# Row scatters and residual traffic handed out over heads and chunks, each behind a one-element copy in GpSimd's queue

## The chip, the cores and the metric

The kernel runs on one core of one Trainium2 chip. The metric is the device time of one execution in microseconds, as the median of several runs. A core has five instruction queues: PE (TensorE, matrix products), DVE (VectorE), ACT (ScalarE), POOL (GpSimd) and SP (SyncE, which here only issues DMAs). POOL issues DMAs too, the indirect ones among them. All DMAs of a core are carried by its 16 DMA engines.

## The reference

The kernel computes one transformer block on 4 sequences of 512 tokens with 512 features (B, S, D). A cross attention comes first, then causal self-attention with 16 heads, then a mixture of 16 experts of which each token takes 6, beside a shared expert. Cut to what matters:

```python
x = x + x_attention(layernorm(x), ctx_1024)        # softmax(q k^T) from ctx alone
h = rmsnorm(layernorm(x), ln1_w)
q, k, v = h @ wq, h @ wk, h @ wv                   # 16 heads of 128
attn = softmax(where(causal, q k^T / sqrt(128), -1e9))
x2 = layernorm(x) + (attn v) @ wo
h2 = rmsnorm(x2, ln2_w)
topv, topi = top_k(softmax(h2 @ gate_w.T), 6)      # topv normalized to sum 1
routed = sum over the 6 experts e of topv_e * (silu(h2 @ eg_e.T) * (h2 @ eu_e.T)) @ ed_e.T
shared = (silu(h2 @ sg.T) * (h2 @ su.T)) @ sd.T
out = x + x2 + routed + shared
```

The residual that ends up in the output is thus the sum of two tensors: `x` after the cross attention (in the kernel `x1`) and `x2` after the self-attention. Its sum is what the change calls the rest.

## The kernel before

**Number format.** Each float32 operand is held as two float16 halves (hi and lo), and each product is three matmuls (`mm3`, lines 83, 86 and 87 of the kernel before).

**Stages.** Batches are called b = 0 to 3. `xattn(b)` is the cross attention, a generator whose pieces are run between other work. The main loop runs over n, one (batch, head) pair per turn, from a list `heads` of 64 pairs. In turn n the queries and keys of head n are made, its scores and softmax follow, and head n-1 is multiplied with its values by `attend`, which leaves `ao` (written by ACT, then by DVE). Two heads form a group; when both are attended, `project` adds their part of the output projection to `x2`. The list goes through batches 0 and 1 in turn, group by group, then through 2 and 3. Batch 0's last heads are 24 and 25, batch 1's 32 and 33, batch 2's 56 and 57, batch 3's 60 to 63.

**Routing.** When a batch's last group is projected, three steps follow. `route1(b)` (same turn) normalizes `x2` tile by tile, splits it into `h2p` (hi by ACT, lo by POOL for batches 0 to 2, line 78), turns it by a DMA transpose (`flip`, line 91, on SP's queue) into `h2T`, and for each of the four tiles does the residual work: load a tile of `x1` from DRAM into `x1t` (one buffer), add `x2`, store it to `r_d` (lines 489, 490, 491, all on POOL). `route2(b)` (two turns later) computes gates, and `route3(b)` (three turns later) the slot of each (token, expert) pair in DRAM, `slotu`, and lists 24 scatters per batch in `scat`: 4 tiles of 128 tokens by 6 experts.

**Scatters.** `scatter(n)` takes up to n entries from that list and issues for each one an indirect DMA from POOL, 128 rows of 2 KB from `h2p` into the expert-sorted array `xs_d` in DRAM (line 455). The main loop calls `scatter(8)` each turn; the last batch's are all issued at once after `route3(B - 1)`. They are declared to be without dependencies among each other, because their slots differ.

**After the loop.** `shared_down(0)`, then `shared(1)`, `shared(2)`: the shared expert in six chunks of up to 128 columns (`gate_up`, leaving `hs`) and a down projection over four tiles (`shared_down`, which adds to `acc`, loaded from `r_d`). `rows_in` then loads rows of `xs_d` by DMA transpose for the first expert, and the 16 experts follow. Results go to `y_d` and are gathered back by indirect DMAs on POOL (line 1105). Batch 3's shared expert stands at the end.

**Order.** A planner with a simulated timeline puts the instructions of each engine in order. `after(b, a)` asks it to keep b behind a on a queue, and `pin` to keep program order. [...] POOL's queue carries, besides the above, the loads of attention weights from their DRAM copies (`fetch`, line 413: `wqk`, `wv`, `wo`), of the shared expert's weights (line 449: `shst`), the stores and loads of `x1` and `hid` (lines 338, 355, 655), and parts of the normalization and routing.

The lines in question, as they stand before:

```python
        scatter(8)
        shared_weights()
...
            x1t = xp.tile([P, D], F32, tag="x1t", name="x1t", bufs=1)
            nc.gpsimd.dma_start(x1t, x1_d[b][:, t, :])
            nc.gpsimd.tensor_tensor(x1t, x1t, x2[:, t, :], ALU.add)
            nc.gpsimd.dma_start(r_d[b][:, t, :], x1t)
```

Of the kernel before, what the change touches and what calls it, by code (L numbers as in the profile page):

```python
# [9 lines left out]
F16 = mybir.dt.float16  # L10
F32 = mybir.dt.float32
# [6 lines left out]
P = 128  # L18
B, S, D = 4, 512, 512
# [36 lines left out]
def xattn_moe_block_kernel(ctx: ExitStack, tc: tile.TileContext, x, xT, ctxT, wqkx, bqk, ln1, ln2,  # L56
# [33 lines left out]
    def flip(o, i):  # L90
        return nc.sync.dma_start_transpose(out=o, in_=i)

    def after(ins, first):
        tc.add_manual_dep(ins.ins, first.ins.name,
                          mybir.DependencyInfo(mybir.DependencyClass.NoSync, mybir.DependencyReason.DATA),
                          reason="order on the queue")
# [341 lines left out]
    def shared_weights():  # L438
# [6 lines left out]
        if pieces:  # L445
# [3 lines left out]
            pin(nc.gpsimd.dma_start(st_, src))  # L449
            loaded.append((dst, st_))  # L450

    def scatter(n):
        while scat and n:
            tt, k = scat.pop(0)
            ins = nc.gpsimd.indirect_dma_start(  # L455
                out=xs_d, out_offset=bass.IndirectOffsetOnAxis(ap=slotu[:, tt, k:k + 1], axis=0),
                in_=h2ps[tt], in_offset=None)
            tc.declare_no_dep(ins.ins, group="scat", reason="the slots differ")
            tc.add_to_no_dep_group("scat", ins.ins)
            scats.append(ins)  # L460
            n -= 1

# [8 lines left out]
    def route1(b, x2):  # L471
        ms = bsm.tile([P, NT], F32, name="rms")
        for t in range(NT):
            sq = xp.tile([P, D], F16, tag="h2", name="rsq", bufs=1)
            nc.scalar.activation(sq, x2[:, t, :], AF.Square, scale=1.0 / math.sqrt(D),
                                 accum_out=ms[:, t:t + 1])
        rr = bsm.tile([P, NT], F32, name="rrs")
        rsqrt(rr, ms, 1e-6)
        h2T[b] = hpool.tile([P, 2 * C, S], F16, tag="hT", name=f"h2T{b}")
        for t in range(NT):  # L480
            tt = b * NT + t
            tl = slice(t * P, (t + 1) * P)
            h2 = xp.tile([P, D], F32, tag="h2", name="h2", bufs=1)
            nc.vector.scalar_tensor_tensor(h2, x2[:, t, :], rr[:, t:t + 1], ln2b, ALU.mult, ALU.mult)
            h2p = h2ps[tt] = rp.tile([P, 2 * D], F16, tag="h2p", name="h2p", bufs=4)
            split1(h2p[:, :D], h2p[:, D:], h2, nc.vector if b == B - 1 else nc.gpsimd)
            zz["flip"] = flip(h2T[b][:, :, tl], h2p)
            x1t = xp.tile([P, D], F32, tag="x1t", name="x1t", bufs=1)
            nc.gpsimd.dma_start(x1t, x1_d[b][:, t, :])
            nc.gpsimd.tensor_tensor(x1t, x1t, x2[:, t, :], ALU.add)  # L490
            nc.gpsimd.dma_start(r_d[b][:, t, :], x1t)

# [180 lines left out]
    def gate_up(b, hid, tmp):  # L673
        shw = shx["w"]
        hs = []
        for ic in range(6):
            R = P if ic < 5 else SR
            if ic % 3 == 0:
                hs.append(hid().rearrange("p (i a s) -> p i a s", i=3, a=2))
            h = hs[-1][:, ic % 3]  # L680

            def proj(ps, a):
                o0 = ic * 8 * P + a * C * P
                mm3(ps, [(shw[:, 0, o0 + c * P:o0 + (c + 1) * P], shw[:, 1, o0 + c * P:o0 + (c + 1) * P],
                          h2T[b][:, c], h2T[b][:, C + c]) for c in range(C)])

            t = tmp()
            pg = bank("a", f"sg{b}_{ic}")
            proj(pg, 0)
            if ic < 5:  # L690
                zz["silu", b, ic] = nc.scalar.activation(t, pg, AF.Silu, scale=PSC)
                pu = bank("w", f"su{b}_{ic}")
                proj(pu, 1)
                nc.vector.scalar_tensor_tensor(t, pu, GS * PSC, t, ALU.mult, ALU.mult)
            else:
                nc.scalar.activation(t[R:], pg[:R], AF.Silu, scale=PSC)
                nc.vector.scalar_tensor_tensor(t[:R], pg[R:], GS * PSC, t[R:], ALU.mult, ALU.mult)
            zz["hs", b] = split1(h[:R, 0], h[:R, 1], t[:R])
            if ic == 5:
                nc.scalar.activation(h[R:2 * R, 0], t[:R], AF.Copy)  # L700
            yield hs

    def store(tt, acc):
        nc.sync.dma_start(out[tt // NT, (tt % NT) * P:(tt % NT + 1) * P, :], acc)

    def shared_down(b, hs, last=False):
        sdw = shx["d"]
        acc = residual(b)
        for t in range(NT):
            tl = slice(t * P, (t + 1) * P)  # L710
            ps = bank("s", f"sy{b}_{t}")
            mm3(ps, [(hs[ic // 3][:, ic % 3, 0, tl], hs[ic // 3][:, ic % 3, 1, tl],
                      sdw[:, 0, ic * D:(ic + 1) * D], sdw[:, 1, ic * D:(ic + 1) * D]) for ic in range(5)], stop=False)
            nc.tensor.matmul(ps, hs[1][:, 2, 0, tl], sdw[:, 0, 5 * D:], start=False, stop=False)
            nc.tensor.matmul(ps, hs[1][:SR, 2, 1, tl], sdw[:SR, 0, 5 * D:], start=False, stop=True)
            nc.vector.scalar_tensor_tensor(acc[:, t], ps, 1.0 / (GS * WS), acc[:, t], ALU.mult, ALU.add)
            if last:
                store(b * NT + t, acc[:, t])

    early = gate_up(0, lambda: ht.tile([P, 2 * NT, S], F16, tag="pt", name="hs0").rearrange("p k s -> p (k s)")[:, :6 * S],  # L720
                    lambda: stg.tile([P, 1024], F32, tag="st", name="sg0")[:, :S])
# [5 lines left out]
        path += [(b + i, g) for g in range(2) for i in range(1, 3) if b + i < B]  # L727
    partner.update((p, q) for p, q in zip(path, path[1:]) if p[1] == q[1])
    heads = [(b, g * HG + j) for b, g in path for j in range(HG)]
    opened = set()  # L730
    left = {b: G for b in range(B)}
    agenda = {}
# [2 lines left out]
    for n in range(NH + LAG + 1):  # L735
        if n < NH:
            b, h = heads[n]
            if b not in opened:
                opened.add(b)
                step(b, 99)  # L740
                if b == B - 1:
                    shared_pool()
            parts = [queries(b, h)]
            if h % HG == 0:
                parts.append(values(b, h // HG))
            if n == 0:
                parts.reverse()
                for p in parts:
                    next(p)
            for p in parts:  # L750
                for _ in p:
                    pass
        m = n - LAG
        if n >= NH:
            for _ in range(3):
                hs0 = next(early)
        if ready:
            b, g = ready.pop()
            project(b, g)
            left[b] -= 1  # L760
            if not left[b]:
                route1(b, x2s[b])
                agenda[n + 2] = agenda[n + 3] = b
                if stop == "B":
                    nc.sync.dma_start(out[b].rearrange("(t p) d -> p t d", p=P), x2s[b])
        if n < NH:
            scores(*heads[n])
        if 0 <= m < NH:
            b, h = heads[m]
            attend(b, h)  # L770
            if h % HG == HG - 1:
                ready.append((b, h // HG))
        if n in agenda and n < NH:
            b = agenda[n]
            if n + 1 in agenda:
                route2(b)
            else:
                route3(b)
        scatter(8)
        shared_weights()  # L780
        if H // 2 <= n < H // 2 + E:
            pad_rows(n - H // 2)
        if n < 6:
            step(1, 2)
        else:
            for _, j in zip(range(2 - n % 2), bring):
                step(j)
    if stop == "B":
        return
    shared_down(0, hs0)  # L790
    bctx.close()
    st2 = ctx.enter_context(tc.tile_pool(name="st2", bufs=2, side="right", reuse_waits="tile"))

    def shared_up(b, tick=lambda: None):
        for hs in gate_up(b, lambda: st2.tile([P, 6 * S], F16, name="hs"), lambda: st2.tile([P, S], F32, name="sgt")):
            tick()
        return hs

    def shared(b):
        shared_down(b, shared_up(b))  # L800

    route2(B - 1)
    route3(B - 1)
    scatter(B * NT * K)

    cps = bank("s", "cnt")
    nc.tensor.matmul(cps[:, :E], onesm, macc, start=True, stop=True)
# [121 lines left out]
    def rows_in(e, h):  # L929
        lo, n = h * CUT, CAPS[e] - CUT if h else CUT  # L930
        t = xts[e, h] = xin.tile([P, 2 * C, n], F16, tag="xT", name="xT")
        flip(t, xs_d[bass.ds(here[e] * T + (1 + lo), n), :])

    seat(0)
    nxt = ranked_weights(0)
    rows_in(0, 0)
    rows_in(0, 1)
    shared(2)

    N = B * NT * K  # L940
    sf, tf = (v.rearrange("p t k -> p (t k)") for v in (slot, tid))
# [185 lines left out]
    def tick():  # L1127
        left = ring["steps"]
        ring["steps"] = max(left - 1, 1)
        for _ in range(-(-len(todo) // left)):  # L1130
            gather()
# [18 lines left out]
    flush()  # L1150
    want(K - 1, yrc, cws, y_d)
    ring["steps"] = 5
    hs = shared_up(B - 1, tick)
    add(0)
    shared_down(B - 1, hs, last=True)
    late.clear()
# [72 lines left out]
```

## Time and profile before

| what | value |
|---|---|
| median of 3 runs | 1832.03 us (1832.01 to 1837.33) |
| profiled execution: time / span | 1838.93 / 1837.2 us |
| PE busy / DVE / ACT / POOL | 1739.6 / 1113.9 / 829.5 / 444.8 us |
| mean granted TensorE clock | 0.974 of full speed |
| `xs_d` scatters (line 455) | 96, 95.3 us of POOL |
| `x1t` loads, adds, stores (lines 489 to 491) | 16 each |
| DMA traffic | 296.23 MB, 161 GB/s on average |

The page of a profile gives busy times of the engines, then the span in 40 equal slices (45.9 us each) with the busy share in tenths, then DMA queues, a chain of waits and groups of instructions. Answers about the trace add a timeline, tables of windows and a list of who waited for whom. In the timeline a line gives start, length, engine, line of the kernel, operation, output and inputs, shapes, a count, and in brackets the idle time before it with what ended it; "issue" there is idle time in which the engine waited for nothing that the profile shows. A busy PE is not a PE at its peak, since the ends of matmuls are modelled. All times of stages below are microseconds from the start of the span.

### The profile page before, as it was taken

How to read it: one execution, taken by the hardware profiler on the slowest of the kernel's cores; microseconds unless marked ns; L12 is line 12 of the kernel's file. 1: busy time of each engine (PE TensorE's matmuls, PEld its weight loads, DVE VectorE, ACT ScalarE, POOL GpSimd, SP SyncE). 2: the span in 40 equal slices, each digit the busy share in tenths (PEclk: the TensorE clock that was granted, in tenths of full speed). 3: DMA queues.
4: the chain of work that ended last, by engine and by line, in shares of the span. 5: the costliest groups of instructions: out<-in, count | busy, mean ns of one | idle time of the engine just before them, and what ended most of it. 6: DMA issues, size and time to landing. Idle time of an engine off the chain costs nothing. (4 is left out here: it accounts for less than half of the span.)

```text
span 1837.2 us, 27581 instructions
## 1 busy us (share of the span) xinstructions
PE 1739.6 (95%) x9919; PEld 937.2 (51%) x9919; DVE 1113.9 (61%) x2766; ACT 829.5 (45%) x1711; POOL 444.8 (24%) x522
## 2 busy tenths in 40 slices
PE   7899999999986998999999979899999999999998
PEld 3455555555543554645655534345555555555453
DVE  6887777777673774756667625554444434446755
ACT  4555645465432543535445423234444444544431
POOL 5423011130345235000003334400000000025564
PEclk9899999999997998999999989899999999999999
DMA  7977768674675677654437534566454655579766
GB/s 235 228 165 215 160 144 191 159 185 93 136 161 159 151 168 212 134 101 91 86 68 150 130 107 102 199 178 177 138 155 144 178 147 147 148 223 252 217 206 209
DMA packets 392723, 296.23 MB, mean 161 GB/s; under 512 B 334880, under 2 KB 335136, under 8 KB 391808
## 3 DMA queue, kind: packets, MB, share of 16 engines
q1 hardware_dynamic: 359456, 180.32, 42.0%
q0 software_dynamic: 33120, 114.06, 19.6%
q8 instruction: 80, 1.31, 0.3%
q14 instruction: 67, 0.55, 0.1%
HBM read 124.81 MB, written 88.94 MB: 116 GB/s over the span
## 5 line engine op out<-in xcount | busy, mean ns | idle before, releaser
L1105 POOL DMA_INDIRECT yg<-y_d,yrc x96 | 110.5, 1151 | 535.8 <-DVE hf L1008 455.6
L630 ACT ACTIVATE pe<-pe,bnm 128x128 f32<-128x128 f32 (+3 forms) x256 | 142.4, 557 | 161.1 <-DVE bnm L628 156.4
L83 PE MATMUL qk<-hT,wqk 128*128 128x512 f16 (+1 forms) x520 | 197.8, 380 | 5.0 <-DMA hT<-hh 3.8
L86 PE MATMUL qk<-hT,wqk 128*128 128x512 f16 (+1 forms) x520 | 197.9, 381 | 1.1 <-issue 1.1
L87 PE MATMUL qk<-hT,wqk 128*128 128x512 f16 (+1 forms) x520 | 197.8, 380 | 1.1 <-issue 1.1
L74 DVE SCALAR_TENSOR_TENSOR pn<-pe,brc,pn 128x128 f16<-128x128 f32 (+3 forms) x256 | 146.7, 582 | 21.9 <-ACT pn L73 18.6
L628 DVE CUSTOM_DVE_ANT_0 pe<-sc,causal 128x128 f32<-128x128 f32 (+3 forms) x256 | 117.4, 486 | 64.0 <-PE sc L625 57.2
L86 PE MATMUL v<-wv,hT 128*128 128x256 f16 x512 | 141.6, 276 | 6.5 <-issue 6.5
L83 PE MATMUL v<-wv,hT 128*128 128x256 f16 x512 | 141.5, 276 | 6.4 <-issue 5.5
L73 ACT ACTIVATE pn<-pe,brc 128x128 f16<-128x128 f32 (+3 forms) x256 | 133.5, 553 | 30.1 <-ACT pe L630 16.3
L87 PE MATMUL v<-wv,hT 128*128 128x256 f16 x512 | 141.5, 276 | 4.9 <-issue 4.7
L83 PE MATMUL g<-xT,wt 128*128 128x384 f16 (+2 forms) x384 | 127.3, 331 | 0.0
L86 PE MATMUL g<-xT,wt 128*128 128x384 f16 (+2 forms) x384 | 127.3, 331 | 0.0
L87 PE MATMUL g<-xT,wt 128*128 128x384 f16 (+2 forms) x384 | 127.2, 331 | 0.0
L994 ACT ACTIVATE hT_e<-hf 128x384 f16<-128x384 f32 (+3 forms) x96 | 51.1, 532 | 143.9 <-DVE hf L1008 136.2
L73 ACT ACTIVATE qkt<-qk 128x512 f16<-128x512 f32 x128 | 75.0, 588 | 90.5 <-PE qk L87 85.0
L83 PE MATMUL y<-dt,hT_e 128*128 128x512 f16 (+1 forms) x288 | 109.4, 380 | 0.0
L87 PE MATMUL y<-dt,hT_e 128*128 128x512 f16 (+1 forms) x288 | 108.9, 378 | 0.0
L86 PE MATMUL y<-dt,hT_e 128*128 128x512 f16 (+1 forms) x288 | 108.9, 378 | 0.0
L662 DVE SCALAR_TENSOR_TENSOR x<-wo,x 128x512 f32<-128x512 f32 x128 | 87.5, 687 | 32.5 <-PE wo L87 31.4
L74 DVE SCALAR_TENSOR_TENSOR qkt<-qk,qkt 128x512 f16<-128x512 f32 x128 | 87.7, 686 | 28.6 <-ACT qkt L73 24.0
L455 POOL DMA_INDIRECT xs_d<-h2p,slotu x96 | 95.3, 993 | 28.2 <-issue 28.2
(320 smaller groups left out, 4019.8 us busy)
## 6 DMA issues: line engine op xcount, KB each, us to landing
y_d<-yt SPq DMA_DIRECT2D x96, 256.0 KB
est<-in_ew_dram SPq DMA_DIRECT2D x32, 704.0 KB
est<-in_ed_dram SPq DMA_DIRECT2D x16, 768.0 KB
wqk<-wqk_d POOLq DMA_DIRECT2D x20, 512.0 KB
wqk_st<-in_wqk_dram SPq DMA_DIRECT2D x16, 512.0 KB
wqk_d<-wqk POOLq DMA_DIRECT2D x15, 512.0 KB
xs_d<-causal POOLq DMA_DIRECT2D x16, 384.0 KB
wv<-wv_d POOLq DMA_DIRECT2D x10, 512.0 KB
```

The source lines that it names most:

```text
L73: return (nc.scalar.activation(hi, src, AF.Copy, scale=scale), nc.vector.scalar_tensor_tensor(lo, src, scale, hi, ALU.mult, ALU.subtract))
L74: nc.vector.scalar_tensor_tensor(lo, src, scale, hi, ALU.mult, ALU.subtract))
L83: ins = nc.tensor.matmul(o, lh, rh, start=start and j == 0, stop=False)
L86: nc.tensor.matmul(o, lh, rl, start=False, stop=False)
L87: ins = nc.tensor.matmul(o, ll, rh, start=False, stop=stop and j == n - 1)
L455: ins = nc.gpsimd.indirect_dma_start(out=xs_d, out_offset=bass.IndirectOffsetOnAxis(ap=slotu[:, tt, k:k + 1], axis=0), in_=h2ps[tt], in_of ...
L628: nc.vector.tensor_tensor_reduce(pe, ps[:, :w], causal[:, S - w:], -1.0, 3e38, ALU.add, ALU.min, nm)
L630: nc.scalar.activation(pe, pe, AF.Exp, bias=nm, scale=-1.0, accum_out=sm)
L662: nc.vector.scalar_tensor_tensor(x2[:, t, :], ps, 1.0 / (VS * WS), x2[:, t, :], ALU.mult, ALU.add)
L994: nc.scalar.activation(hT[:R, ic, :w], hf, AF.Copy)
L1105: nc.gpsimd.indirect_dma_start(out=yg, out_offset=None, in_=src, in_offset=bass.IndirectOffsetOnAxis(ap=idx[:, tt, k:k + 1], axis=0))
```

## The change

Three things are done. First, `pace(src)` puts a copy of one element into POOL's queue, from a tile that another engine writes into a tile `mark`, and asks the planner to keep it behind the last scatter or mark; `scatter` and the `x1` load ask to be kept behind the last mark in turn. Second, the residual work leaves `route1`: each (batch, tile) is put on a list `rest`, and `rest_step` does one of them per turn of the main loop; what is left after the loop is done tile by tile in `shared_down(0)`. Third, the scatters of a turn are no longer 8 but the number left, divided by the turns until the next batch ends (`ends`); batch 3's are handed out two per chunk and per tile in `shared(1)` and `shared(2)` (`drip`), and the remaining ones, with the loads of the first expert's rows, are issued after the second chunk of `shared(2)`. The mark of turn n reads `ao` of head n-2.

```diff
@@ -449,6 +449,14 @@
             pin(nc.gpsimd.dma_start(st_, src))
             loaded.append((dst, st_))
 
+    mark = const.tile([1, 1], F16, name="mark")
+
+    def pace(src):
+        ins = nc.gpsimd.tensor_copy(mark, src)
+        if scats:
+            after(ins, scats[-1])
+        scats.append(ins)
+
     def scatter(n):
         while scat and n:
             tt, k = scat.pop(0)
@@ -457,6 +465,8 @@
                 in_=h2ps[tt], in_offset=None)
             tc.declare_no_dep(ins.ins, group="scat", reason="the slots differ")
             tc.add_to_no_dep_group("scat", ins.ins)
+            if scats:
+                after(ins, scats[-1])
             scats.append(ins)
             n -= 1
 
@@ -485,8 +495,17 @@
             h2p = h2ps[tt] = rp.tile([P, 2 * D], F16, tag="h2p", name="h2p", bufs=4)
             split1(h2p[:, :D], h2p[:, D:], h2, nc.vector if b == B - 1 else nc.gpsimd)
             zz["flip"] = flip(h2T[b][:, :, tl], h2p)
+            rest.append((b, t, x2))
+
+    rest = []
+
+    def rest_step():
+        if rest:
+            b, t, x2 = rest.pop(0)
             x1t = xp.tile([P, D], F32, tag="x1t", name="x1t", bufs=1)
-            nc.gpsimd.dma_start(x1t, x1_d[b][:, t, :])
+            ins = nc.gpsimd.dma_start(x1t, x1_d[b][:, t, :])
+            if scats:
+                after(ins, scats[-1])
             nc.gpsimd.tensor_tensor(x1t, x1t, x2[:, t, :], ALU.add)
             nc.gpsimd.dma_start(r_d[b][:, t, :], x1t)
 
@@ -703,7 +722,7 @@
     def store(tt, acc):
         nc.sync.dma_start(out[tt // NT, (tt % NT) * P:(tt % NT + 1) * P, :], acc)
 
-    def shared_down(b, hs, last=False):
+    def shared_down(b, hs, last=False, tick=lambda src: None):
         sdw = shx["d"]
         acc = residual(b)
         for t in range(NT):
@@ -716,6 +735,7 @@
             nc.vector.scalar_tensor_tensor(acc[:, t], ps, 1.0 / (GS * WS), acc[:, t], ALU.mult, ALU.add)
             if last:
                 store(b * NT + t, acc[:, t])
+            tick(acc[0:1, t, 0:1])
 
     early = gate_up(0, lambda: ht.tile([P, 2 * NT, S], F16, tag="pt", name="hs0").rearrange("p k s -> p (k s)")[:, :6 * S],
                     lambda: stg.tile([P, 1024], F32, tag="st", name="sg0")[:, :S])
@@ -727,6 +747,7 @@
         path += [(b + i, g) for g in range(2) for i in range(1, 3) if b + i < B]
     partner.update((p, q) for p, q in zip(path, path[1:]) if p[1] == q[1])
     heads = [(b, g * HG + j) for b, g in path for j in range(HG)]
+    ends = [max(i for i, (b, _) in enumerate(heads) if b == j) + LAG + 1 for j in range(B)]
     opened = set()
     left = {b: G for b in range(B)}
     agenda = {}
@@ -776,7 +797,11 @@
                 route2(b)
             else:
                 route3(b)
-        scatter(8)
+        if m > 0 and (rest or scat):
+            pace(aos[heads[m - 1][0], heads[m - 1][1] // HG][0:1, heads[m - 1][1] % HG, 1, 0:1])
+        rest_step()
+        if scat:
+            scatter(-(-len(scat) // max(1, min(x for x in ends if x > n) - n)))
         shared_weights()
         if H // 2 <= n < H // 2 + E:
             pad_rows(n - H // 2)
@@ -787,21 +812,33 @@
                 step(j)
     if stop == "B":
         return
-    shared_down(0, hs0)
+
+    def rest_tick(src):
+        if rest:
+            pace(src)
+            rest_step()
+
+    shared_down(0, hs0, tick=rest_tick)
     bctx.close()
     st2 = ctx.enter_context(tc.tile_pool(name="st2", bufs=2, side="right", reuse_waits="tile"))
 
-    def shared_up(b, tick=lambda: None):
-        for hs in gate_up(b, lambda: st2.tile([P, 6 * S], F16, name="hs"), lambda: st2.tile([P, S], F32, name="sgt")):
-            tick()
-        return hs
-
-    def shared(b):
-        shared_down(b, shared_up(b))
+    def up(b):
+        return gate_up(b, lambda: st2.tile([P, 6 * S], F16, name="hs"), lambda: st2.tile([P, S], F32, name="sgt"))
+
+    def drip(src):
+        if scat:
+            pace(src)
+            scatter(2)
+
+    def shared(b, first=lambda: None):
+        for ic, hs in enumerate(up(b)):
+            drip(hs[ic // 3][0:1, ic % 3, 0, 0:1])
+            if ic == 1:
+                first()
+        shared_down(b, hs, tick=drip)
 
     route2(B - 1)
     route3(B - 1)
-    scatter(B * NT * K)
 
     cps = bank("s", "cnt")
     nc.tensor.matmul(cps[:, :E], onesm, macc, start=True, stop=True)
@@ -933,9 +970,7 @@
 
     seat(0)
     nxt = ranked_weights(0)
-    rows_in(0, 0)
-    rows_in(0, 1)
-    shared(2)
+    shared(2, lambda: (scatter(B * NT * K), rows_in(0, 0), rows_in(0, 1)))
 
     N = B * NT * K
     sf, tf = (v.rearrange("p t k -> p (t k)") for v in (slot, tid))
@@ -1150,7 +1185,8 @@
     flush()
     want(K - 1, yrc, cws, y_d)
     ring["steps"] = 5
-    hs = shared_up(B - 1, tick)
+    for hs in up(B - 1):
+        tick()
     add(0)
     shared_down(B - 1, hs, last=True)
     late.clear()
```

## The prediction

> **What bounds the kernel now.** I read the page first (part 1, the slices of part 2, the queues of part 3), then tables of windows, then the timeline where they show a hole.
>
> ```profile
> PE 1739.6 (95%) x9919; PEld 937.2 (51%) x9919; DVE 1113.9 (61%) x2766; ACT 829.5 (45%) x1711; POOL 444.8 (24%) x522
> ...
> PE   7899999999986998999999979899999999999998
> ...
> POOL 5423011130345235000003334400000000025564
> PEclk9899999999997998999999989899999999999999
> ...
> q8 instruction: 80, 1.31, 0.3%
> ```
>
> TensorE sets the time; a microsecond is won only where its row is under 9 or its clock under 9. Those slices are where POOL is busy, around 490 to 600, 690 to 730, 1010 to 1080 and 1110 to 1180 us. To price them I added up, in windows of 10 us, the columns of the matmuls in TensorE's timeline at 2,400 a microsecond (512-column matmuls start 0.216 us apart in quiet stretches) and took the rest as shortfall. Over 560 to 590 it is 8.5 + 8.8 + 5.7 = 23.0 us; over 690 to 730, 16.5; over 1050 to 1080, 15.2; over 1160 to 1180, 10.4. These four, 65 us, are the four row-scatter bursts (batches 0 to 3). Beside the route1 calls before them: 490 to 530, 13.2; 650 to 670, 2.2; 1010 to 1030, 4.2; 1110 to 1130, 3.0. The columns of the table below are the window, its length, busy us of PE, PEld, DVE, ACT and POOL, PE clock, DMA share and GB/s.
>
> ```profile
> 555.00:560.00 5.00, 5.00 (x37) 3.29 (x35) 3.65 (x14) 2.94 (x7) 3.78 (x5) 1.00 0.62 234
> 560.00:565.00 5.00, 1.09 (x6) 0.38 (x4) 0.34 (x1) 0.00 (x0) 3.78 (x5) 0.99 1.03 225
> 565.00:570.00 5.00, 2.81 (x10) 1.08 (x10) 0.20 (x1) 0.60 (x1) 4.21 (x5) 0.50 0.69 255
> ...
> 575.00:580.00 5.00, 1.52 (x5) 0.41 (x4) 0.00 (x0) 0.00 (x0) 3.78 (x5) 0.50 0.56 210
> 580.00:585.00 5.00, 2.83 (x14) 1.65 (x14) 0.96 (x2) 1.03 (x2) 0.29 (x1) 0.50 0.19 72
> ```
>
> PE, DVE and ACT all run dry while POOL alone works: no engine waits for another. The timeline says what POOL does, and what TensorE waits for:
>
> ```profile
> 574.10 0.37 PE L86 MATMUL v<-wv,hT 128*128 128x256 f16 x1 [0.33 <-issue]
> 574.81 0.37 PE L87 MATMUL v<-wv,hT 128*128 128x256 f16 x1 [0.33 <-issue]
> 576.21 0.37 PE L83 MATMUL v<-wv,hT 128*128 128x256 f16 x1 [1.03 <-issue]
> ```
> ```profile
> 574.30 0.96 POOL L455 DMA_INDIRECT xs_d<-h2p,slotu  x1 [0.30 <-issue]
> 575.56 0.96 POOL L455 DMA_INDIRECT xs_d<-h2p,slotu  x1 [0.30 <-issue]
> ```
>
> "Issue" means that no wait of the program is open: the instruction itself is late. One scatter goes out every 1.27 us (128 rows of 2 KB, 256 KB); 24 run from 548.9 to 580.3. TensorE starves from 560.3, 11.5 us after the first, to 584.3; then 4 us pass at half clock. [...] The other bursts starve TensorE 8.5, 13.7 and 23.6 us after their first scatter.
>
> [...]
>
> **The change part by part.** What counts is the order in which the built program puts things in GpSimd's queue, and it is not what the source suggests. By the source, batch 0's scatters go 5, 5, 5, 5, 4 over five heads, batch 1's 2, 2, 2 and then one a head, batch 2's 8, 8, 8, batch 3's two a chunk. In the built queue the marks are in order, but only the first scatter behind each mark stays there: scatters belong to a group without mutual dependencies, so the order asked for between two of them is lost, and the others are hoisted. Found: batch 0 is 5, mark, 16, then three marks with one each; batch 1 is 2, mark, 3, mark, then one a mark; batch 2 is 8, mark, 13, mark, 3; batch 3 is 2, mark, 12, then ten marks with one each. The marks inside the runs of batches 0 and 2 wait for nothing new.
>
> *Batch 1* (16.5 us): the first five share about 10 us with two 512 KB weight loads, the other 19 come one per head (13.4 us). The shortest delay to starvation seen is 8.5 us, so no backlog forms; 1.5 us left: **-15** (ends -8 and -17).
> *Batch 0* (23.0): 21 still run together. Three fewer save 3.8 us of burst; one L353 (0.76), one mark and two DMA issues (0.55 each) put between them give 2 back: **-2** (-8, +5).
> *Batch 2* (15.2): likewise 21, nothing put between: **-3** (-8, +8).
> *Batch 3* (10.4): 14 together; the next four marks wait for chunks whose hs ACT ended by 1146.6, before their turn near 1160, and acc's first two for 1153. So some 20 to 22 run through, a mark between the last: **-2** (-10, +8). The last two scatters wait for chunks 0 and 1 of shared(2), and the first expert's transposing loads (xs_d, at 1189.7 now) wait for them. Cover: shared(2)'s up part takes some 30 us, the first expert matmul stands at 1210; last scatter near 1175, 3 us to land, two loads of 3.2 us: **0**.
> *Residual traffic.* Now h2p's low halves leave POOL at 489.8, 495.5, 501.2 and 506.9, since each stands behind an x1t round trip in the queue:
>
> ```profile
> POOL x1t L489 <- DMA r_d<-x1t: 34.8, 15, 7.1
> ...
> POOL x1t L490 <- DMA x1t<-x_d: 25.0, 11, 2.9
> ```
> ```profile
> PE av L83 <- DMA pt<-pn: 11.6, 6, 5.5
> ```
>
> h2T's flips wait for h2p, the pt flips stand behind them on SP's queue, and TensorE waits 5.5 us for one at 523, then runs at half clock. One x1t step per head takes the round trips out: four h2p at about 2.8 us (batch 2's last ones are 2.7 apart) end near 498, 9 us earlier, and the 1 MB x<-hid_d load leaves 506 for about 535. The mark ahead of the second h2p waits for an ao finished at 489.5: no delay. Of 13.2 us: **-7** (-12, +5 if that mark is late). Smaller holes after it, 9.4 us: **-2** (-4, +3). The load that moves is next needed by project(2,0), near 575.
> *Marks*: 54 copies of one element; the trace has none, the nearest row is macc at 0.22 us. 12 us on an engine that is idle 76%: **0**. What they hold: the L413 weight loads behind them. *Scatters between heads*: 19 times 256 KB beside weight loads and flips at a DMA share of 0.4 to 0.6: **+2** (0, +6). TensorE's own order also shifts in places, before any mark too: unknown, 0 (-4, +4).
>
> Sum: -15 - 2 - 3 - 2 - 7 - 2 + 2 = **-29 us**. Against the profiled execution, 1838.9 (span 1837.2 and 1.7 around it), that is 1809.9; the median of the runs, 1832.0, stands 6.9 lower, and I carry the difference over: **1803**.
>
> **Rivals.** *The change does what it says*, because marks wait longer than I think and break all four bursts: of 65 us some 55 go, with 9 of residual: 1832 - 62 = 1770, or 1785 if half holds. Against: the built order. Chance 0.14. *Only the phase counts*: [...] If the three remaining bursts each cost 23 like batch 0's (0, +8, +13) and batch 1 and the residual give 24, the result is 1829. For: the delays of 8.5 to 23.6 us. Chance 0.13. *Slower: marks hold weight loads.* A wo load is issued at 853.2 when its buffer comes free and used at 868.5; less 4 us for landing, 11 us of slack. A mark waits for the head two back, one per 13.4 us, so a load placed one mark too late can miss it. At 18 us held, 7 us are lost in each of six group pairs: 42 - 28 = +14, 1846. It decides the sign from 16 us on. Against: the planner put marks between loads, not several ahead of one. Chance 0.10.
>
> **How the numbers follow.** My case has 0.63 and by itself spans 1790 to 1818. A measurement of this kernel tells some 0.3% (5.5 us) from no change. Faster: 0.63 + 0.14 + 0.04 of the phase case = 0.81; same: 0.09; slower: 0.10. The range 1780 to 1831 leaves out the full first rival and the slower one.
>
> **What would show it.** Right: 19 single L463 scatters over heads 39 to 58, no issue gaps there; runs of some 21 in batches 0 and 2 with PE at 0.50 behind them; h2p spaced about 3 us; no 5.5 us wait for pt. Wrong: issue gaps in batch 1's stretch; no starvation in batch 0's; PE waiting for wqk, wv or wo.

## The result and the profile after

The changed kernel takes 1807.7 us (median of 4 runs, 1805.6 to 1813.9), the kernel before beside it 1833.7 (1832.0 to 1837.3): ratio 0.986, 95% interval [0.983, 0.989]. The profiled execution's span went from 1837.2 to 1804.3 us. The forecast was 1803. Medians here and below are of all runs and ratios of the faster of the two states in which runs of one kernel fall, so a difference of medians can be a few microseconds larger than the ratio says.

First the page of the changed kernel: busy time of each engine, then tenths in 40 slices of 45 us.

```profile
PE 1730.2 (96%) x9919; PEld 935.9 (52%) x9919; DVE 1112.3 (62%) x2766; ACT 830.3 (46%) x1711; POOL 467.4 (26%) x576
...
PE   7899999999998999999999799899999999999998
...
POOL 5423011130256252121113624300000000025654
```

TensorE's matmuls are the same; its busy time is 9.4 us shorter, and of the 32.9 us that the span lost 23.5 were idle time. POOL's row had 5 0 0 0 0 0 from slice 15 (counted from 0) on; now 5 2 1 2 1 1 1 stand from slice 14 on: batch 1's scatters are spread over its heads. In PE's row the 8, 6 of slices 11 and 12 and the 8 of slice 15 have become a single 8 at 12. The 7 and the 8 of batches 2 and 3 (slices 22 and 25; before 23 and 25) have stayed.

Batch 0's burst in the windows of the changed kernel (columns as before: window, length, busy time of PE, PEld, DVE, ACT and POOL, PE clock, DMA share, GB/s):

```profile
555.00:560.00 5.00, 1.95 (x9) 0.82 (x8) 1.78 (x3) 1.19 (x2) 4.21 (x6) 0.79 1.09 297
560.00:565.00 5.00, 4.42 (x22) 2.51 (x21) 0.32 (x2) 0.60 (x1) 3.94 (x5) 0.53 0.86 275
565.00:570.00 5.00, 3.29 (x19) 1.56 (x17) 0.44 (x1) 0.05 (x1) 3.93 (x5) 1.00 0.66 269
570.00:575.00 5.00, 3.28 (x9) 1.31 (x9) 2.06 (x10) 2.39 (x8) 1.07 (x2) 0.66 0.26 105
```

POOL issues as densely as before, and PE still runs dry, but less deeply: its poorest 5 us hold 1.95 busy where before's held 1.09. Batch 1's heads, in POOL's timeline of the changed kernel:

```profile
719.84 1.04 POOL L455 COPY mark<-ao 1x1 f16<-1x1 f16 x1 [5.83 <-DVE ao L74]
721.05 1.03 POOL L463 DMA_INDIRECT xs_d<-h2p,slotu  x1 [0.17 <-issue]
...
722.64 0.53 POOL L413 DMA_DIRECT2D wqk<-wqk_d  x1
```

A mark waits for a head's ao, one scatter follows it, and the weight load behind goes out at once. While it waits, from 714.0 to 719.8, POOL starts nothing of what stands behind it. From 690 to 870 no 10 us of TensorE fall short by over 0.65. Three waits of the changed kernel (total, times, longest):

```profile
PE av L83 <- DMA pt<-pn: 8.1, 6, 2.4
...
POOL x1t L506 <- DMA r_d<-x1t: 7.1, 2, 4.9
...
POOL x1t L509 <- DMA x1t<-x_d: 36.2, 11, 5.3
```

GpSimd's wait for the store of the x1t before is down from 34.8 us to 7.1, and TensorE's longest wait for a pt flip from 5.5 to 2.4. The other half of the round trip, the wait of the add for its load, has grown from 25.0 to 36.2; it now falls between heads, and no weight load behind it reached TensorE late.

To put places of different kernels side by side I cut the run by TensorE's completed work (its matmul columns at 2,400 a microsecond, the rate taken in the prediction, 1% over the 512 in 0.216 us that quiet stretches show; added up from the timeline) and not by time. Each entry is the time that TensorE took for a stage beyond its work at this rate, in us of one profiled execution; where exactly a stage is cut moves an entry by up to 1 us:

| stage, by work done | before | after | forecast of the difference |
|---|---|---|---|
| route1(0) and batch 0's burst (400 to 525) | 38.4 | 18.5 | -9 |
| next heads (525 to 600) | 3.5 | 4.5 | |
| batch 1's burst (600 to 660) | 17.7 | 2.7 | -15 |
| heads after it (660 to 740) | 8.6 | 1.7 | -2, of all smaller holes |
| route1(2) and batch 2's burst (905 to 970) | 17.4 | 20.0 | -3 |
| route1(3) and batch 3's burst (970 to 1035) | 14.4 | 15.6 | -2 |
| shared(2)'s end and first expert (1035 to 1110) | 2.7 | 6.0 | 0 |
| all else | 73.6 | 74.4 | +2 |
| sum | 176.3 | 143.5 | -29 |

### The profile page after: what moved, and what is told of

The parts are those of the page before. It is cut to its first block, busy times and chain, and to the rows that moved or that the text cites. A ratio compares the mean times of both kernels' runs of the same rounds, so it can differ in the third digit from the quotient of the medians.

```text
span 1804.3 us, 27676 instructions
## 1 busy us (share of the span) xinstructions
PE 1730.2 (96%) x9919; PEld 935.9 (52%) x9919; DVE 1112.3 (62%) x2766; ACT 830.3 (46%) x1711; POOL 467.4 (26%) x576
## 3 DMA queue, kind: packets, MB, share of 16 engines
q8 instruction: 80, 1.31, 0.3%
## 5 line engine op out<-in xcount | busy, mean ns | idle before, releaser
L74 DVE SCALAR_TENSOR_TENSOR pn<-pe,brc,pn 128x128 f16<-128x128 f32 (+3 forms) x256 | 145.6, 579 | 21.9 <-ACT pn L73 16.8
L74 DVE SCALAR_TENSOR_TENSOR qkt<-qk,qkt 128x512 f16<-128x512 f32 x128 | 87.6, 686 | 20.8 <-ACT qkt L73 16.8
```

The lines of the kernel that those rows point to most:

```text
L74: nc.vector.scalar_tensor_tensor(lo, src, scale, hi, ALU.mult, ALU.subtract))
```

## The experiments

They ran in three sets, each on one chip, with the kernel before timed beside it. Its median was 1794.4 in the first set, 1844.4 in the second and 1797.4 in the third. This difference, larger than the change, became the main finding; it is called one between chips below, though each chip was used in one set only, so the chip and the time of the set are not told apart. A ratio below is always to the kernel before of the same set.

The theory (A) is: a dense run of scatters makes instructions come late, and the change gains by breaking runs and by taking the residual round trips out of route1. Rivals: the residual alone gains (B); only the phase counts, that is, which place of the program TensorE has reached when a run begins (C); held loads eat the gain (D). E, F and G came up on the way and are told where they are first expected. In the code below, `...` stands for what is not shown.

### The residual handed out, no marks (first set)

```diff
-        if m > 0 and (rest or scat):
-            pace(aos[...])
         rest_step()
-        if scat:
-            scatter(-(-len(scat) // max(1, ...)))
+        scatter(8)
```

The after() lines of rest_step, scatter and drip go too, and the last scatters and rows_in stand where they did before.

> Only the residual traffic is handed out, one x1t step a head; the scatters stand as in the kernel before, in four runs of 24. Theory A [...]: the stretch 510 to 530 loses about 3 us where before it lost 13, the four bursts keep 15 to 23 us each, so some 1824 against 1834, ratio 0.993 to 0.996. Rival B (the round trips of the residual are most of the gain): 1812 or less, ratio under 0.990. Rival C [...]: burst losses change by 5 us or more each in either direction though their lengths are the same; the time may be anywhere from 1815 to 1845.

Measured 1794.4 against 1794.4, ratio 0.999 [0.997, 1.001]. No theory had it. The traces explain it: without a mark all five queues come out as in the kernel before, instruction for instruction. The planner put the steps back where they were, so this run is the kernel before on another chip and says nothing of the residual. The wait for pt is still there (TensorE's waits from 400 to 700):

```profile
PE av L83 <- DMA pt<-pn: 11.4, 5, 5.6
```

What the run does show is that the bursts, 24 scatters at 1.27 us as before, starve next to nothing on this chip. Batch 0's runs from 554.5 to 585.2; its windows, in the same columns:

```profile
575.00:580.00 5.00, 5.00 (x29) 2.52 (x27) 4.42 (x14) 3.60 (x9) 3.78 (x5) 1.00 0.89 257
580.00:585.00 5.00, 5.00 (x25) 2.25 (x23) 3.37 (x8) 0.60 (x1) 4.02 (x4) 1.00 1.01 267
```

PE is full and its clock is 1.00, while POOL issues a scatter every 1.27 us and the DMA share is 0.89 to 1.01. So a full set of DMA engines does not by itself stop TensorE.

### The scatters handed out, no residual (first set, and once more in the third)

```diff
             rest.append((b, t, x2))
+            x1t = xp.tile([P, D], F32, tag="x1t", name="x1t", bufs=1)
+            nc.gpsimd.dma_start(x1t, x1_d[b][:, t, :])
+            nc.gpsimd.tensor_tensor(x1t, x1t, x2[:, t, :], ALU.add)
+            nc.gpsimd.dma_start(r_d[b][:, t, :], x1t)
+            rest.pop()
```

> The scatters and marks of the kernel after, the residual traffic inside route1 as before. Theory A: batch 1's burst gone (-15), batch 0's shortened (-10), the hole of 13 us at 490 to 530 back: about 1812, ratio 0.986 to 0.991, and together with the residual kernel the two gains should add to that of the whole change (26 us). Rival B: little of the gain is left, 1825 or more.

Measured 1787.4, ratio 0.9975 [0.9951, 0.9998]: 4 to 5 us less by the ratio, hardly clear of noise. Theory A's 0.986 to 0.991 is missed; the first experiment's trace, which is the kernel before on this chip, had little starvation to remove.

### Every scatter held by a mark (first set)

```diff
+        marks.append(ins)            # in pace
...
-            if scats:
-                after(ins, scats[-1])
+            if marks:
+                after(ins, marks[-1])  # in scatter
```

> As the kernel after, but every scatter is ordered behind the latest mark instead of behind the scatter before it, so GpSimd's queue holds 5, mark, 5, mark, 5, mark, 5, mark, 4 (batch 0), 8, mark, 8, mark, 8 (batch 2) and 2 a mark (batch 3). Theory A: batch 0's loss of 13 us falls to 3 or less, batch 2's 18 to about 5, batch 3's 7 to about 4: 20 to 26 us less, some 1784, ratio to before 0.972 to 0.978. Rival C (phase, not length): the stretches move up and down without a trend, 1800 to 1812. Rival D (the marks that now wait hold the loads behind them): waits of TensorE for wqk, wv or wo of over 3 us, time at or above 1810.

In the built queue batch 0 is now 5, 5, 5, 5, 4 with marks between and batch 2 8, 8, 8. The order between two scatters had been what was lost; asked of a mark, it holds. Measured 1785.3, ratio 0.993 [0.991, 0.995]. Theory A's 0.972 to 0.978 missed again, and rival D shows itself at one place. POOL's timeline, then TensorE's:

```profile
545.80 0.96 POOL L466 DMA_INDIRECT xs_d<-h2p,slotu  x1 [0.30 <-issue]
546.77 0.60 POOL L413 DMA_DIRECT2D wqk<-wqk_d  x1
```

```profile
557.99 0.61 PE L83 MATMUL qk<-hT,wqk 128*128 128x512 f16 x1 [7.11 <-DMA wqk<-wqk_d]
```

The wqk load stands behind ten scatters, is issued at 546.8, and TensorE waits 7.1 us for it. This is the slower rival of the prediction, at one head and not at six group pairs. The heads behind batch 0's burst took 16.0 us beyond their work here, but not for a load held by a mark: 11.5 of them are a wait for a pt flip that went out at 585.7, beside four scatters and a wv load, and landed at 602.5. The DMA share was 1.17 from 588 to 600. A share of 1.01 did not slow TensorE in the first experiment, but here this transfer took 16.8 us.

### No marks at all (first set)

```diff
     def pace(src):
-        ins = nc.gpsimd.tensor_copy(mark, src)
-        if scats:
-            after(ins, scats[-1])
-        scats.append(ins)
+        return
```

> The hand-out by heads and chunks without any mark. The built queue then has runs of 24 for batches 0, 2 and 3 and 2, 2, 7, 9, 4 for batch 1. Theory A: the time of the kernel with the residual alone, within 6 us: 1818 to 1830. If spreading in the source did the work without marks: 1806 to 1811, as the kernel after.

Measured 1791.7, ratio 0.998 [0.996, 1.001]: as the first experiment, within 3 us, though both lie under the times expected. The queue has runs of 24 for batches 0, 2 and 3 and 2, 2, 7, 9, 4 for batch 1. Handing out in the source does nothing without a mark.

### The kernel before, once more (second set)

> The kernel before, unchanged, for a trace beside the others of this set. The first set ran on another chip than the two first traces, with the kernel before at 1794 instead of 1834, and there the same bursts of 24 scatters left TensorE's instructions at their usual pace (no gaps of 0.7 us). Theory E (the late instructions belong to the chip, not to the burst): on a chip where the kernel takes 1790 to 1800 the trace has under 10 us of gaps of 0.55 to 0.95 us between TensorE's instructions, where the first trace has 40; on one where it takes 1830 or more they are back. Theory A as first held [...]: 30 us or more of them in any case.

Measured 1845.1 (one execution). The late instructions are back. I counted gaps of 0.55 to 0.95 us between the starts of TensorE's instructions, weight loads and semaphore steps included: they add up to 40.5 us in the first trace of before and 27.7 here, against 7.6 in the first experiment, whose bursts are the same. The place is the same as well. In both traces of before the 6,280th instruction of TensorE is the first late one, at 560.5 and 562.7, 11.6 to 11.7 us after the first scatter. In the first experiment TensorE passes that instruction 11.2 us after the first scatter, 0.11 us apart from its neighbours as in quiet stretches.

### The changed kernel, once more (second set)

> The changed kernel, unchanged, timed beside the kernel before on the chip of this set. Theory A: 26 us less, ratio 0.983 to 0.989, on any chip. Theory E: on a chip without late instructions only the residual traffic (about 10) and the loads and flips that no longer stand behind 24 scatters are won, ratio 0.990 to 0.996.

Measured 1804.9 against 1844.4, ratio 0.982 [0.977, 0.987]: some 34 us less by the ratio (40 by the medians), where the first pair had 26; the two intervals overlap. Of the stages, batch 1's burst goes from 18.1 to 2.8 us and route1(0) with batch 0's burst from 37.5 to 19.6, which is nearly the first pair's difference again (-15.3 and -17.9). Batch 2's burst stays (18.0, 16.6), and shared(2)'s end with the first expert loses as in the first pair.

### Two marks a head (second set)

```diff
+        if scat and 0 < n <= NH:
+            pace(qks[heads[n - 1]][0][0:1, 0, 0:1])
+            dose(n, 0)
...
-            scatter(-(-len(scat) // max(1, ...)))
+        dose(n, 1)
```

dose() divides what is left by the number of marks to come; every scatter is held by the latest mark, as in "Every scatter held by a mark".

> Every scatter ordered behind the latest mark, and two marks a head (one on the query tile of the head before, one on ao), so that 3, 3, 3, 3, 3, 3, 2, 2, 2 scatters of batch 0, one or none of batch 1 and 5, 5, 5, 5, 4 of batch 2 stand between marks. In the kernel with every scatter held and one mark a head, TensorE waited 7.5 us at 550 for a wqk load that stood behind ten scatters and 11.7 us at 591 for a wv load behind four. Theory: no load then stands behind more than 3 scatters (4 us), both waits fall under 4 us, some 10 us less than that kernel: ratio to before 0.984 to 0.990. Rival: twice the marks hold the loads as long, waits stay, 0.991 to 0.996.

Measured 1797.3 (1794.5 to 1800.9), ratio 0.977 [0.972, 0.981]: better than the expected 0.984 to 0.990 (the expectation was laid out for a smaller loss before), 7 us under the changed kernel and 47 under the kernel before by the medians (some 43 by the ratio), though its interval still overlaps the changed kernel's. Both waits of the kernel with every scatter held are gone, the 7.1 and the 11.5 us. But batches 0 and 2 still lose 17.0 and 18.9 us in their stages, and POOL's timeline says why, here for batch 2:

```profile
1008.87 0.96 POOL L466 DMA_INDIRECT xs_d<-h2p,slotu  x1 [0.30 <-issue]
...
1010.78 0.18 POOL L455 COPY mark<-ao 1x1 f16<-1x1 f16 x1
1011.12 1.03 POOL L466 DMA_INDIRECT xs_d<-h2p,slotu  x1 [0.15 <-issue]
```

The mark between two groups takes 0.18 us and waits for nothing. GpSimd reaches batch 2's scatters after the head that the mark reads has long ended, so 24 scatters run from 997 to 1028 with one pause of a microsecond. In batch 0, 18 scatters run from 538 to 564 before a mark waits. To stand in the right order is not enough; what the mark reads has to end late.

### Every scatter twice (second set)

```diff
-            ins = nc.gpsimd.indirect_dma_start(out=xs_d, ...)
+            for dst in (xs_d, xz_d):
+                ins = nc.gpsimd.indirect_dma_start(out=dst, ...)
```

> The kernel before with every scatter issued a second time into an unused tensor, so that a burst is 48 long, 61 us. Theory A [...]: starvation starts in each burst at the latest some 25 us in and lasts to its end, 30 us a burst or 120 in all, time over 1880. Theory E on a chip without late instructions: no gaps of 0.7 us even so; only loads and flips behind the longer run cost, 10 to 40 us in all.

Measured 2003.2 (one execution): 159 us more than the kernel before of this set, for 96 scatters more, or 1.65 us for each. Beyond their work the four burst stages lost 66.7, 56.3, 49.9 and 51.8 us against 37.5, 18.1, 18.0 and 13.1. Windows of the first burst (552 to 613) and behind it:

```profile
590.00:600.00 10.00, 2.53 (x5) 0.63 (x6) 1.15 (x2) 0.60 (x1) 7.56 (x9) 0.50 0.54 206
600.00:610.00 10.00, 2.07 (x4) 0.31 (x3) 0.00 (x0) 0.00 (x0) 7.56 (x9) 0.50 0.54 204
...
620.00:630.00 10.00, 9.91 (x46) 4.61 (x46) 8.52 (x29) 6.43 (x16) 0.59 (x1) 0.86 0.21 43
```

TensorE is busy for 2 to 2.5 of 10 us, with four or five matmuls, for as long as scatters go out, and is back at 9.91 once they have ended. DVE and ACT stand nearly still with it. The DMA share meanwhile is 0.54, half of what the first experiment showed with TensorE full. TensorE's timeline there:

```profile
592.15 0.37 PE L627 MATMUL sc<-qkt,qkt 128*128 128x256 f16 x1 [1.70 <-issue]
593.57 0.60 PE L625 MATMUL sc<-qkt,qkt 128*128 128x512 f16 x1 [1.04 <-issue]
```

No wait of the program is open, and starts here are 1.42 to 2.81 us apart, multiples of some 0.70 (weight loads take the steps between). This is theory A in its plainest form: on this chip each further scatter of a run costs TensorE about its own 1.27 us (29 to 39 us for the 30.5 us added to a burst). Twice the scatters are also twice their traffic, so length and bytes are not told apart, and the doubling was not run on a chip without late instructions.

### Two marks a head, with gaps between the scatters (third set)

```diff
+            gap = nc.gpsimd.tensor_tensor(mark[:, :3], mark[:, :3], mhalf[:, :3], ALU.pow)
+            after(gap, ins)
+            marks.append(gap)
...
```

> The kernel with two marks a head, and behind every scatter a small power on GpSimd (some 1.2 us, on a tile that nobody needs), so that scatters stand 2.5 us apart instead of 1.27. In the kernel with two marks a head the marks of batches 0 and 2 did not wait, so 18 and 24 scatters still ran together and the stretches 550 to 580 and 1010 to 1040 lost 11.9 and 17.1 us. Theory A ([...] it needs them dense as well as many): no gaps of 0.7 us left in these stretches, some 3 and 5 us lost, about 20 us less than that kernel, ratio to before 0.962 to 0.970 where the kernel before takes over 1830. Rival F (the time that scatters run counts, not how dense they are): starvation sets in 10 to 20 us after the first and lasts twice as long, ratio 0.985 or more. Rival G (loads and the next h2p behind the longer run take it back): waits of TensorE for wqk, wv, h2T grow by 10 us or more, ratio 0.972 to 0.980.

The kernel before with the same gaps:

> The kernel before with nothing changed but the small power behind every scatter: runs of 24 at 2.5 us instead of 1.27, 60 us long. Where the kernel before takes over 1830: theory A expects the 65 us of the four bursts to fall under 25, with 10 to 20 us of waits for weight loads and h2p that now stand in the longer runs: ratio 0.982 to 0.992. Rival F expects 1.000 to 1.03. Where the kernel before takes under 1800 there is nothing to win, ratio 1.000 to 1.010 under either.

Measured 1803.5, ratio 1.004 [1.002, 1.006], and 1814.9, ratio 1.009 [1.005, 1.013]. This chip again has no late instructions (their gaps add up to 8.7 us at most in any kernel of the first and third set), so the two, whose scatters stood about 2.3 us apart within a run (the power took some 0.9 us in the first, 1.0 in the second), could not tell density from length. That stays open. They do price a longer run. TensorE's waits in the first and then in the second (total, times, longest):

```profile
PE g L83 <- DMA xT<-xs_d: 11.5, 1, 11.5
```

```profile
PE av L83 <- DMA pt<-pn: 30.4, 9, 12.4
```

Batch 3's scatters end at 1166 in the first of these, the first expert's xT loads go out at 1168.9, and TensorE waits 11.5 us; in the first experiment's trace it does not wait for them. In the second, waits for pt cost 30.4 us where the first experiment's trace has 16.5.

### The residual behind its marks (third set)

```diff
-        if m > 0 and (rest or scat):
+        if m > 0 and rest:
             pace(...)
         rest_step()
-        if scat:
-            scatter(-(-len(scat) // max(1, ...)))
+        scatter(8)
```

The after() of scatter and the work of drip go too.

> The residual half of the change alone, with its marks; the scatters go as in the kernel before. My part sums: the hole at 490 to 530 falls from 13 us to about 3, batch 0's h2p come some 6 us earlier, the bursts stay: 10 us less, ratio 0.992 to 0.996. If the residual is the larger part of the gain: under 0.990.

The other half beside it, the same kernel as in the second experiment:

> The scatter half alone, with its marks, once more. On a chip where the kernel before takes over 1830: batch 1's burst gone (-15) and batch 0's cut (-5 to -10), ratio 0.984 to 0.990; with the residual half it should add up to the whole change within 6 us. On one under 1800: as in its first run, 0.995 to 1.000.

Measured 1783.8, ratio 0.993 [0.990, 0.995], for the residual; 1788.8, ratio 0.996 [0.993, 0.998], for the scatters, which agrees with their first run. Against the first experiment's trace, which has the same queue as before on such a chip, the residual with marks saves 6.2 us in the heads after batch 1's burst (8.1 to 1.9). The scatters save 3.8 us in batch 1's own stage (6.7 to 2.9) and the same 6 us behind it (8.1 to 2.1), and give 3.9 back at the first expert (2.6 to 6.5). So on a chip without late instructions the residual measured the larger half, some 13 us against 8 by the ratios (4 in the scatters' first run), though the two intervals overlap.

Of the residual's gain the trace places little. At route1(0) and batch 0's burst, where the prediction had 7 us of it, it saves nothing here (15.7 us lost, 16.0 in the first experiment's trace): the wait at route1 is gone, but in and around the run of 24 scatters TensorE waits for pt flips again (527 to 596: total, times, longest).

```profile
PE av L83 <- DMA pt<-pn: 7.5, 3, 5.0
```

Where instructions come late, the first pair's table has 15 us in batch 1's stage alone, which I put down to the scatters; neither half was run on such a chip, so there the gain is not divided by experiment.

## Why the prediction was right, and where it was not

The sum owes part of its fit to luck: of -29 forecast and -33 found between the two profiled executions, the single terms missed by 17 us to one side and 13 to the other.

**Batch 1, -15: right**, in size and place. 17.7 fell to 2.7, and again 18.1 to 2.8 on the second set's chip, and TensorE's issue gaps there went from 8.3 us to 0.7. On a chip without late instructions the scatters' half of the edit is worth 4 us there.

**Batch 0 and route1(0), -2 and -7: too small.** -19.9 in place of -9. The wait for pt (5.5 us, then a granted clock of 0.55 over 520 to 525) went as worked out (1.2 us and 1.00 are left of it), though the last h2p ended 5.6 us earlier (502.5) and not 9: the window 490 to 530 holds 3.0 where it held 13.2, or -10.2. The other mis-sized term is batch 0's burst: over 550 to 580 it lost 13.4 us, where 560 to 590 had lost 23.0, so -9.6 against -2 (and beyond its end at -8). I priced three scatters fewer and some work put between. In place of that the trace shows that TensorE's lateness starts later and ends earlier: it begins 14.4 us after the first scatter (540.4 to 554.8; 11.7 before) and its dense part is over at 562.6, 7 us ahead of the run's last scatter, where before it outlasted the run by 4 us. The second set repeats it (19.6 against 37.5 for the stage). The other engines did not get off so early. ScalarE and VectorE of the changed kernel stood idle up to the run's end, for the times in brackets:

```profile
569.95 0.60 ACT L73 ACTIVATE vt<-v 128x512 f16<-128x512 f32 x1 [5.24 <-remote]
```

```profile
571.37 0.29 DVE L647 CUSTOM_DVE_ANT_0 pe<-sc,causal 128x128 f32<-128x128 f32 x1 [5.93 <-remote]
```

TensorE's last gap there, 3.0 us from 568.7, ends as VectorE is back. Whether the small pauses in the run (hd and a mark at 547, ioe and a wqk load at 556 to 560, a store at 562), the run's other place in the program, or something else shortened the loss was not tried.

**Batch 2, -3: not there.** The first pair has +2.6, the second set -1.4 (18.0 to 16.6), one execution each, so no change can be read from them. The built order was read rightly (24 scatters, 1004.7 to 1035.8, with marks that hardly wait), but I gave the kernel credit for three scatters behind a second mark. That mark hardly waited either, and the three scatters followed at once. The two-marks run shows it again.

**Batch 3 and the seam, -2 and 0: wrong, +1.2 and +3.3.** 22 scatters ran through, as I had it, and the last two waited for chunks; TensorE never waited for xT. The term that failed is the seam's 0, the way from the last scatter to xT. I priced xT's cover and not what stands behind xT on SP's queue: est loads (weights of the experts) and the load of acc for shared(2)'s down part. SP's timeline, VectorE's and TensorE's:

```profile
1155.24 11.35 SPq L91 DMA_TRANSPOSE xT<-xs_d  x3
1166.86 1.04 SPq L915 DMA_DIRECT2D est<-in_ew_dram  x2
...
1168.55 0.64 SPq L689 DMA_DIRECT2D acc<-r_d  x1
```

```profile
1176.56 1.76 DVE L74 SCALAR_TENSOR_TENSOR dt<-est,dt 128x1536 f16<-128x1536 f32 x1 [0.37 <-ACT dt L73]
1178.35 1.89 DVE L735 SCALAR_TENSOR_TENSOR acc<-sy,acc 128x512 f32<-128x512 f32 x3
```

```profile
1179.09 0.58 PE L83 MATMUL sy<-sdw,hs 128*128 128x512 f16 x1 [2.50 <-DVE acc L735]
```

est and acc are issued about 1 us of TensorE's work later than before (acc with 1,051 of its 1,660 us of work done, then 1,050). VectorE splits what est brought, adds to acc at once behind it, from 1178.35, and a matmul of sy waits 2.5 us behind that, where before it waited 0.7. That is 1.8 of the 3.3. Of the other traces with batch 3's scatters handed out behind marks, four have 2.8 to 3.8 us of this wait, the one with two marks a head has 1.2, and the one with gaps waits for xT instead. Where the scatters run together it is 1.4 at most. What moves est and acc was not taken apart: SP's waits have 0.8 us of xT for scatters in this trace, but none in the second set's trace of the same kernel, which loses the same.

**Smaller holes, -2: too small, -6.9** in the heads behind batch 1's burst. Before, one matmul of av came 4.0 us late:

```profile
805.65 0.58 PE L83 MATMUL av<-pt,vt 128*128 128x512 f16 x1 [4.02 <-issue]
```

In spite of "issue" it is not a late instruction: in the trace's records TensorE's sequencer stands in a semaphore wait from 798.6 to 805.6, and what ends it is a pt flip that SP had issued at 795.95. In the first experiment's trace, the same program, this flip took 10.2 us to land (771.2 to 781.4). A wqk, a shst and a wv load left POOL around it, within 5.3 us (794 to 799), with a DMA share of 1.30. In the changed kernel, and in either half alone with its marks, these loads stand further apart and the stage loses about 2 us. But in the kernel without marks the three leave within 5.2 us as well, the flip lands in 4.5 us and the hole is not there. So three loads close together are not enough for it, and what makes the flip slow stays open. No term of mine had it.

**Marks, 0 and "spread scatters", +2: about right** (+0.8 in all else). Marks waited 149.7 us for ao, and TensorE waited for no weight load behind them in this kernel. In the kernel with every scatter held, a load came 7.1 us late, so the slower rival is real at another dose.

**The rival "only the phase counts"** is not ruled out as a part: in batch 0's runs lateness starts 11 to 16 us in, in the kernel before at one and the same instruction each time, in the changed kernel some 20 to 30 instructions later. But doubling the scatters adds 29 to 39 us to each of the four burst stages, which where it starts cannot do.

**The mechanism.** That more scatters in a run make more instructions late is shown, by doubling, on a chip where it happens. By what means they do it is not shown. Full DMA engines alone are not it: with TensorE full the DMA share was 1.04 (first experiment, 565 to 570), with TensorE starved 0.54 (every scatter twice). The page of before has two DMA queues of the kind "instruction", q8 with 80 packets in 1.31 MB and q14, which the prediction passed over, with 67 in 0.55 MB; the pages of the first experiment and of the second set's kernel before have the same figures. In the trace's records the packet of q8 inside batch 0's burst took 0.92 to 1.43 us in the traces where TensorE starves and 0.93 where it doesn't (first experiment); over the whole run of before such packets took 0.88 to 2.02. It comes at the same place of TensorE's work (the 6,320th to 6,330th instruction), in before at 575.6, 15 us after the first late instruction, so it does not begin the stall. A packet of q14 comes within 0.5 us of TensorE's first late instruction in all three traces of the kernel before's order on chips where it happens (560.8, 563.1 and 564.0), but the first experiment has the same packet at the same place, and nothing is late there; batch 1's burst has none near its start. What makes the instructions late stays open, as does why the chips differ with the same instructions and the same scatters: the gaps of 0.55 to 0.95 us add up to 27.7 us in the second set's kernel before and to 8.7 at most in any kernel of the other two sets.

The forecast therefore held for a chip like that of the first trace. On the other kind the two halves measured some 13 and 8 us by their ratios. Both remove the same 6 us behind batch 1's burst, so together I would expect less than the sum; the whole change was not run there.

## What to carry to other kernels

Read the order in the built queue: a hand-out in the source is worth nothing if the planner can undo it, and a mark paces only if what it reads ends later than the queue would get there (one waited 5.83 us among batch 1's heads of the changed kernel, one not at all among batch 2's scatters with two marks a head). When loads are moved behind something, price all that is behind them on the same queue, to the next user. Before explaining a hole by the program, see whether another chip's trace of the same program has it. And before calling an instruction late, see whether the sequencer in front of it stands in a wait.

## What the hardware showed that was not expected

The same kernel has medians of 1794, 1797, 1834 and 1844 us in four settings. The difference lies in the burst stages: between the first experiment (133.8 us beyond the work) and the second set's kernel before (183.4), two traces with the same instructions in the same order, the four stages of route1 and bursts differ by 52 us and all else by -2. On such a chip late instructions come one or two at a time, 0.70 us apart or a multiple of it, on TensorE, while VectorE and ScalarE stand nearly still (0.00 to 1.15 and 0.00 to 0.60 us busy of 10, every scatter twice, 580 to 610) and GpSimd keeps issuing a scatter every 1.27 us.
